# A four-layer graph network on one core: row sums of four node tiles in 32 moved to DMA, and one step of the first layer's opening moved by a unit

## The chip, the core and the metric

The kernel runs on one core of a Trainium2 chip. A core has five engines with queues of their own: PE (matrix products), DVE (vector operations), ACT (scalar functions), POOL (GpSimd) and SP (here only a queue for transfers). They run side by side and wait for each other by semaphores. Sixteen DMA engines move data between memory and the core's SBUF, fed from the queues of SP, ACT and POOL. The metric is the device time of one execution in microseconds (us). It is the median of the runs shown.

## What is computed

4096 nodes with 256 features go through four layers, each a sort of attention over the same 4096 x 4096 adjacency matrix, each followed by a residual sum and a layer norm. The change concerns the first layer:

```python
def _L0_gnn_ref(h, adj, W, a):
    Wh = (h @ W).reshape(n, heads, d)                       # 4 heads of 64
    s_i = jnp.einsum('nhd,hd->nh', Wh, a[:, :d])
    s_j = jnp.einsum('nhd,hd->nh', Wh, a[:, d:])
    e = s_i[:, None, :] + s_j[None, :, :]
    e = jax.nn.leaky_relu(e, negative_slope=0.2)
    e = jnp.where((adj == 0)[:, :, None], -jnp.inf, e)
    alpha = jax.nn.softmax(e, axis=1)
    out = jnp.einsum('ijh,jhd->ihd', alpha, Wh).reshape(n, heads * d)
    return jax.nn.elu(out)
...
x = _layernorm(x + _L0_gnn_ref(x, adj, L0_gnn_W, L0_gnn_a), axis=-1)
x = _layernorm(x + _L1_gnn_ref(...), axis=-1)
x = _layernorm(x + _L2_gnn_ref(...), axis=-1)
x = _layernorm(x + _L3_gnn_ref(...), axis=-1)
```

The weight of an edge, exp(leaky_relu(s_i + s_j)), is the larger of exp(s_i + s_j) and exp(0.2 (s_i + s_j)). A factor that depends on the row i alone drops out of the softmax. Divided by exp(0.2 s_i) it is max(exp(0.8 s_i) exp(s_j), exp(0.2 s_j)), and exp(0.2 s_j) can also be taken out of the maximum: exp(0.2 s_j) max(exp(0.8 s_i) exp(0.8 s_j), 1).

## The kernel before

**Tiles and units.** The first layer is `additive_heads`. The nodes are cut into 32 tiles of 128 (`NT`) and 8 blocks of 512 (`NB`). For a block b of rows i and a node tile j there is one unit; the loop runs over all 256 units, blocks outermost. In a unit `weights(b, j)` makes a buffer `prob` of 128 nodes j by 4 heads by 512 rows i, 1 MB in all, and `sums(b, j)` multiplies it into the block's accumulators in PSUM. `sums` follows `weights` two units later in the program (`LAG`).

**Weights.** `row[b]` holds exp(0.8 s_i) of the block's rows on all partitions, `dst` holds exp(0.8 s_j). ACT makes Relu(row x dst - 1) for each head, four operations of 128x512 (L299). DVE then adds 1 and multiplies by the edge mask for all heads, one operation of 128x2048 (L302). The mask of two units is one transfer of 512 KB on SP's queue (L295). The buffers `prob` come from the pool `zp`, which has eight.

**Sums.** `V` holds the projected features times exp(0.2 s_j), and exp(0.2 s_j) itself in its last four columns. PE holds 32 columns of V for each head and moves `prob` through: for each of three groups n four products, one a head, into 32 output partitions each (L312). Groups 0 and 1 give the features, group 2 (n = HC) takes the last columns, spread over 32 columns, and gives the row sums. A product of these 32-bit numbers leaves two records in the trace. At the end of a block ACT and DVE copy the three accumulators into `kept` (L317). In the next block's units `finish` transposes them (`turned`, L324), divides by the row sums and does elu, the residual and the layer norm (`outputs`, `add_elu` with `neg` on DVE and ACT in turn, L229 to L231).

**First block.** While it runs, `turn` transposes the next blocks' input and `prepare` projects it (`additive_values`): products L215, three exponentials on ACT (L219 to L221), and the scaled V on DVE (L222), in a group of three node tiles and a group of one. `prepare(0)`, the rows of block 0 and `turn(1)` stand ahead of the loop. After unit 0 come `turn(2)` and `prepare(1)`; from unit 3 on every fourth unit prepares one more block.

**Other queues.** Every eighth unit (j = 4, 12, 20, 28) `narrow` has POOL copy one column of that unit's `prob` into `tick` (L90) and then issue a transfer that stores a part of the adjacency matrix as bytes (`edges`, L1349). Only the second layer reads it. `rows` (L281 to L288) makes the row of the block after next by two transfers on SP's queue.

**Order.** PE's order is the program's (`manual_schedule`). In this layer a scheduler orders the other engines by the data's ways. The later layers, `multi_head_attention`, `additive_one` and `cosine_attention`, are not touched. The second layer sums its row sums in part by accumulating transfers from POOL (`den`, L873), and that is where its entries in the profile come from.

Of the kernel before, what the change touches and what calls it, by code (L numbers as in the profile page):

```python
# [9 lines left out]
FP = mybir.dt.float32  # L10
# [3 lines left out]
AF = mybir.ActivationFunctionType  # L14
OP = mybir.AluOpType
# [3 lines left out]
P = 128  # L19
D = 256  # L20
KC = D // P
QB = 4
QW = QB * P
# [5 lines left out]
def kernel(  # L29
# [27 lines left out]
    nc = tc.nc  # L57
    N = x.shape[0]
    NT = N // P
    NB = N // QW  # L60

    def pool(stack, name, bufs, **kw):
        return stack.enter_context(tc.tile_pool(name=name, bufs=bufs, reuse_waits="tile", **kw))
# [8 lines left out]
    ones = const.tile([P, P], FP, name="ones")  # L72
# [29 lines left out]
    def attach(pl, w_sb, a_sb, H):  # L102

        d = D // H
        for c in range(KC):
            prod = pl.tile([P, H, 2, d], FP, name="prod")
            nc.vector.tensor_tensor(prod, w_sb[:, c, :D].rearrange("p (h d) -> p h d", h=H).unsqueeze(2)
                                    .to_broadcast([P, H, 2, d]), a_sb.rearrange("p (h n d) -> p h n d", h=H, n=2), OP.mult)
            nc.vector.tensor_reduce(w_sb[:, c, D:].rearrange("p (n h) -> p h n", h=H), prod, AX.X, OP.add)
# [95 lines left out]

    def additive_values(xT, b, groups, w_sb, V, src, dst, H, slope):

        g = 1.0 - slope  # L210
        heads = "p k (h d) -> p k h d"
        for k, n, pw in groups:
            for c in range(KC):
                for i in range(n):
                    nc.tensor.matmul(pw[:, i, :D + 2 * H], xT[:, c, k + i], w_sb[:, c, :],  # L215
                                     start=(c == 0), stop=(c == KC - 1))
            t = slice(b * QB + k, b * QB + k + n)
            s, d = pw[:, :, D:D + H], pw[:, :, D + H:D + 2 * H]
            nc.scalar.activation(src[:, t, :], s, AF.Exp, scale=g)  # L219
            nc.scalar.activation(dst[:, t, :], d, AF.Exp, scale=g)  # L220
            nc.scalar.activation(V[:, t, D:], d, AF.Exp, scale=slope)  # L221
            nc.vector.tensor_tensor(V[:, t, :D].rearrange(heads, h=H), pw[:, :, :D].rearrange(heads, h=H),  # L222
                                    V[:, t, D:].unsqueeze(3).to_broadcast([P, n, H, D // H]), OP.mult)

# [10 lines left out]
    def additive_heads(a, H, slope, early, narrow, ahead):  # L235


        d = D // H
        G = P // H
        HC = H // 2  # L240
        MJ = 2
        mvs, kept = {}, {}
        with ExitStack() as lay:
            keep = pool(lay, "ga_keep", 1)
            V = keep.tile([P, NT, D + H], FP, name="V")
            src = keep.tile([P, NT, H], FP, name="src")
            dst = keep.tile([P, NT, H], FP, name="dst")
            w_sb = keep.tile([P, KC, D + 2 * H], FP, name="w0_sb")
# [3 lines left out]
            load_w(w_sb[:, :, :D], w0, nc.scalar)  # L252
            load_x(1)
            rp = pool(lay, "ga_row", 2)
            zp = pool(lay, "ga_z", 8)
            sb = pool(lay, "ga_sb", 2)
            mp = pool(lay, "ga_mask", 4)
            dr = pool(lay, "ga_dram", 2, space=bass.MemoryType.DRAM)
            ps = pool(lay, "ga_ps", 2, space=PSUM)
            pa = pool(lay, "ga_pa", 2, space=PSUM)  # L260
            edges = adjT.rearrange("(t p) i -> p t i", p=P)
            row, mask, acc, prob = {}, {}, {}, {}

            def bank():
                return ps.tile([P, QW], FP, name="g")
# [9 lines left out]
            def keep_rows(banks):  # L275
                for h in range(H):
                    (nc.vector.tensor_copy if h % 2 else nc.scalar.copy)(row[0][:, h, :], banks[h])
# [13 lines left out]
            def weights(b, j, rows=None):  # L291
                m = b, j // MJ
                if j % MJ == 0:
                    mask[m] = mp.tile([P, MJ, QW], I32, name="mask")
                    nc.sync.dma_start(mask[m], edges[:, j:j + MJ, b * QW:(b + 1) * QW])  # L295
                z = prob[b, j] = zp.tile([P, H, QW], FP, name="prob")
                for h in range(H):
                    r = rows[h] if rows else row[b][:, h, :]
                    nc.scalar.activation(z[:, h, :], r, AF.Relu, bias=-1.0, scale=dst[:, j, h:h + 1])  # L299
                if rows:  # L300
                    keep_rows(rows)
                nc.vector.scalar_tensor_tensor(z, z, 1.0, mask[m][:, j % MJ, :].unsqueeze(1).to_broadcast([P, H, QW]),  # L302
                                               OP.add, OP.mult)

            def sums(b, j):
                if j == 0:
                    acc[b] = pa.tile([P, HC + 1, QW], FP, name="acc")
                for n in range(HC + 1):
                    for h in range(H):
                        lo = h * d + n * G  # L310
                        part = V[:, j, lo:lo + G] if n < HC else V[:, j, D + h:D + h + 1].to_broadcast([P, G])
                        nc.tensor.matmul(acc[b][h * G:(h + 1) * G, n, :], part, prob[b, j][:, h, :],  # L312
                                         start=(j == 0), stop=(j == NT - 1))
                if j == NT - 1:
                    kept[b] = [fin1.tile([P, QW], FP, name=f"kept{c}") for c in range(HC + 1)]
                    for c in range(HC + 1):
                        (nc.vector.tensor_copy if c == 1 else nc.scalar.copy)(kept[b][c], acc[b][:, c, :])  # L317
                    mvs[b] = fin.tile([P, QB, 2], FP, name="mv")
# [35 lines left out]
            def turn(b, bank=bank):  # L354
                if b + 2 < NB:
                    load_x(b + 2)
                busy = (nc.scalar.copy if b == 0 else nc.vector.tensor_copy,
                        nc.vector.tensor_copy if b == 1 else nc.scalar.copy)
                xTs[b] = transposed_block(sb, bank, b, busy)

            def prepare(b):
                groups = [(0, HC + 1, side), (HC + 1, 1, bank().rearrange("p (n f) -> p n f", n=1))]
                additive_values(xTs[b], b, groups, w_sb, V, src, dst, H, slope)

            pos, roots, xTs = {}, {}, {}
            LAG = 2
            units = [(b, j) for b in range(NB) for j in range(NT)]
            with tc.manual_schedule(engines={mybir.EngineType.PE}):


                over = pa.tile([P, HC + 1, QW], FP, name="acc")
                side = pa.tile([P, HC + 1, QW], FP, name="acc")

                def warm(n):

                    for _ in range(n):
                        nc.tensor.matmul(over[:, 0, :P], ones, ones, start=True, stop=True)

                warm(2)
                nc.tensor.matmul(side[:, 0, :], ones[:1, :], a_row, start=True, stop=True)  # L380
                attach(keep, w_sb, side[:, 0, :], H)
                turn(0)
                warm(2)
                prepare(0)
                banks = [bank()] + [over[:, h, :] for h in range(H - 1)]
                first_rows(banks)
                free = iter([side[:, 0, :], side[:, 1, :]])
                turn(1, lambda: next(free))
                for i in range(len(units) + LAG):
                    if i < len(units):  # L390
                        b, j = units[i]
                        weights(b, j, None if i else banks)
                        if (b, j) == (1, 4 * QB):
                            early()
                        if i % 8 == 4:
                            narrow(prob[b, j][:, 0, :1])
                    if i >= LAG:
                        b, j = units[i - LAG]
                        sums(b, j)
                        if b:  # L400
                            finish(b - 1, j)

                    if i == 0 or i % QB == 3 and 3 + i // QB <= NB:
                        b = 1 if i == 0 else 2 + i // QB
                        if b + 1 < NB:
                            turn(b + 1)
                        prepare(b)
                        if b == 3:
                            rows(1, bank())
                    if i == (NB - 1) * NT + 20:  # L410
                        ahead(bank)
# [299 lines left out]
    def multi_head_attention(w_sb, b_sb, tail, rows_of_den, rows_done, narrow_edges, ga):  # L711
# [7 lines left out]
        G = P // H  # L719
        MJ = 4  # L720
        NH = N // d
# [317 lines left out]
    class Cosine:  # L1039

        MJ = 4
# [321 lines left out]
    with ExitStack() as weights1, ExitStack() as den1, ExitStack() as weights3:  # L1363
# [19 lines left out]
        def ahead(bank):  # L1383
            bm_sb["x"] = transposed_block(wp, bank, 0)
# [42 lines left out]
```

## Time and profile before

| | us |
|---|---|
| median of 3 runs | 2785.65 (2785.55 to 2785.95) |
| the profiled execution | 2785.99 |
| its span, first to last instruction | 2784.2 |
| first layer's sums on PE | 19.9 to 723.3 |
| one block of the first layer, from the second on | 84.4 |

The block's time is the distance between the first `kept` transposes of neighbouring blocks on PE, which start at 397.5 and 481.9 us. On the page each engine's first figure is the time in which it was busy. PE's weight loads (PEld) lie beside its products. A group's line gives the busy time, the mean duration in ns, then the engine's idle time ahead of it and what ended that. Durations of instructions that follow at once overlap by some 90 ns, so counts times means are more than the busy time. The tensor clock was granted at 0.999 of full speed.

### The profile page before, as it was taken

The page shows a single profiled execution, that of the slowest core. Times are in us where ns is not written, and L with a number is a line of the kernel's source. Part 1 is how long each engine was busy: PE and PEld are TensorE (multiplying, and loading weights), DVE is VectorE, ACT ScalarE, POOL GpSimd, SP SyncE. Part 2 cuts the span into 40 slices and gives each one's busy share as a digit, 9 for nine tenths or more (in the row PEclk, how much of TensorE's full clock was granted, in tenths as well). Part 3 has the DMA queues.
Part 4 walks back from the last instruction along what each step waited for, and adds up shares of the span by engine and source line. Part 5 has one row for each costly group of instructions (what it writes and reads, how often), then busy time and mean ns, then how long its engine had stood idle before and what let it go on. Part 6 is the DMA issues. An engine that isn't in the chain of part 4 may idle for free. (4 is left out here: it accounts for less than half of the span.)

```text
span 2784.2 us, 50486 instructions
## 1 busy us (share of the span) xinstructions
PE 2768.9 (99%) x19557; PEld 1449.1 (52%) x19557; DVE 2299.5 (83%) x3049; ACT 1703.4 (61%) x2668; POOL 1080.8 (39%) x1020
## 2 busy tenths in 40 slices
PE   9999999999999999999999999999999999999999
PEld 5333333333453333333333335888888777777776
DVE  8899999999677788887888878888887866777776
ACT  8899999999336666666666666465565422222222
POOL 0000100100029878778787887455455000000000
PEclk9999999999999999999999999999999999999999
DMA  7566676665339899998989988567777545445442
GB/s 207 107 142 137 139 145 124 140 143 119 69 98 192 185 176 196 193 187 186 192 181 189 190 183 188 175 197 214 186 209 230 121 69 83 76 77 83 75 72 43
DMA packets 275066, 411.94 MB, mean 148 GB/s; under 512 B 54809, under 2 KB 155657, under 8 KB 273930
## 3 DMA queue, kind: packets, MB, share of 16 engines
q0 software_dynamic: 104176, 182.74, 41.5%
q1 hardware_dynamic: 164280, 218.88, 26.2%
q10 hardware_dynamic: 6370, 7.10, 0.8%
q8 instruction: 153, 2.51, 0.4%
q14 instruction: 87, 0.71, 0.1%
HBM read 335.94 MB, written 39.40 MB: 135 GB/s over the span
## 5 line engine op out<-in xcount | busy, mean ns | idle before, releaser
L857 DVE TENSOR_TENSOR prob<-p,mask 128x1024 f32<-128x1024 f32 x512 | 619.3, 1222 | 165.3 <-ACT p L847 158.5
L847 ACT ACTIVATE p<-p,shift 128x1024 f32<-128x1024 f32 x512 | 555.5, 1087 | 319.9 <-PE p L845 318.9
L312 PE MATMUL acc<-prob,V 128*32 128x512 f32 x6144 | 664.0, 592 | 1.1 <-DVE prob L302 1.1
L299 ACT ACTIVATE prob<-row,dst 128x512 f32<-128x512 f32 x1020 | 635.0, 713 | 0.6
L302 DVE SCALAR_TENSOR_TENSOR prob<-prob,mask 128x2048 f32<-128x2048 f32 x256 | 580.3, 2285 | 25.8 <-ACT prob L299 25.1
L867 POOL TENSOR_TENSOR den<-den,prob 128x1024 f32<-128x1024 f32 x220 | 557.8, 2535 | 92.9 <-DVE prob L857 82.7
L845 PE MATMUL p<-qT,kT 64*64 64x512 f32 x4096 | 531.1, 590 | 2.6 <-DVE prob L857 2.6
L881 PE MATMUL acc<-prob,V 64*64 64x512 f32 x4096 | 529.9, 589 | 0.0
L312 PEld LDWEIGHTS acc<-prob,V 128*32 128x32 f32 x6144 | 197.3, 110 | 453.0 <-issue 431.3
L453 PE MATMUL acc<-mix,mixed 128*128 128x256 f32 x1476 | 401.4, 380 | 2.0 <-DVE quarters L475 1.0
L881 PEld LDWEIGHTS acc<-prob,V 64*64 64x64 f32 x4096 | 157.4, 133 | 282.2 <-issue 280.3
L453 PEld LDWEIGHTS acc<-mix,mixed 128*128 128x128 f32 x1476 | 278.5, 190 | 45.6 <-PE acc L453 3.1
L845 PEld LDWEIGHTS p<-qT,kT 64*64 64x64 f32 x4096 | 154.3, 133 | 279.6 <-issue 253.3
L90 POOL COPY tick<-prob 128x1 f32<-128x1 f32 x35 | 38.0, 1085 | 642.7 <-DVE prob L302 641.7
L1154 DVE TENSOR_TENSOR prob<-prob,mask 128x1024 f32<-128x1024 f32 x128 | 156.3, 1221 | 142.9 <-ACT prob L1145 142.9
L873 POOL DMA_DIRECT2D den<-prob x240 | 230.5, 961 | 61.9 <-DMA den<-prob 25.4
L453 PE MATMUL acc<-prob,X 128*128 128x256 f32 x984 | 252.6, 379 | 0.0
L1073 POOL DMA_DIRECT2D mask<-in_adjT x64 | 47.6, 743 | 526.9 <-DVE prob L1154 508.3
L453 PEld LDWEIGHTS acc<-prob,X 128*128 128x128 f32 x984 | 186.7, 190 | 78.8 <-issue 59.2
L586 DVE SCALAR_TENSOR_TENSOR prob<-r,own,mask 128x512 f32<-128x512 f32 x252 | 177.0, 743 | 48.4 <-POOL mix L445 11.4
L1145 ACT ACTIVATE prob<-p 128x512 f32<-128x512 f32 x144 | 86.1, 598 | 212.5 <-PE p L1141 212.5
L1145 ACT ACTIVATE prob<-g 128x512 f32<-128x512 f32 x112 | 66.9, 597 | 199.3 <-PE g L1141 199.3
(239 smaller groups left out, 2845.1 us busy)
## 6 DMA issues: line engine op xcount, KB each, us to landing
mask<-in_adjT SPq DMA_DIRECT2D x254, 512.0 KB
den<-prob POOLq DMA_DIRECT2D x240, 512.0 KB, 5.2
mask<-edges SPq DMA_DIRECT2D x512, 64.0 KB
mask<-in_adjT POOLq DMA_DIRECT2D x64, 512.0 KB, 5.6
edges<-in_adj POOLq DMA_DIRECT2D x32, 512.0 KB, 9.9
far<-squares SPq DMA_DIRECT2D x16, 512.0 KB
den<-prob SPq DMA_DIRECT2D x16, 512.0 KB
row<-far SPq DMA_DIRECT2D x7, 1024.0 KB
```

Of the source, the lines that this page charges most:

```text
L299: nc.scalar.activation(z[:, h, :], r, AF.Relu, bias=-1.0, scale=dst[:, j, h:h + 1])
L302: nc.vector.scalar_tensor_tensor(z, z, 1.0, mask[m][:, j % MJ, :].unsqueeze(1).to_broadcast([P, H, QW]), OP.add, OP.mult)
L312: nc.tensor.matmul(acc[b][h * G:(h + 1) * G, n, :], part, prob[b, j][:, h, :], start=(j == 0), stop=(j == NT - 1))
L453: nc.tensor.matmul(acc[at][:, half * HW:(half + 1) * HW], w, a, start=(g == 0 and n in (0, 2, 3, 5)), stop=(g == NP - 1), skip_group_check ...
L586: nc.vector.scalar_tensor_tensor(z[:, n, :], r, ga.own[:, j:j + 1], mask[:, n, :], OP.add, OP.mult)
L845: nc.tensor.matmul(p[c * d:(c + 1) * d, r, :], kT[half, c, at:at + d], qT[half, c, cols], start=True, stop=True)
L847: nc.scalar.activation(p, p, AF.Exp, bias=shift)
L857: nc.vector.tensor_tensor(z, p, mask[m][:, j % MJ, :].unsqueeze(1).to_broadcast([P, KC, QW]), OP.mult)
L867: nc.gpsimd.tensor_tensor(to, to, flat, OP.add)
L873: nc.gpsimd.dma_start(to, flat, accum_op=OP.add)
L881: nc.tensor.matmul(acc[b][c][r * d:(r + 1) * d, :], V[half, j, r * d:(r + 1) * d], prob[b, j][half, r, :], start=(j == 0), stop=(j == NH - 1))
L1154: nc.vector.tensor_tensor(z, z, co.mask[b, 2 * g // MJ][:, lo:lo + 2, :], OP.mult)
```

## The change

Four node tiles (`APART`: 3, 11, 19, 27) are treated apart.

- Their exp(0.2 s_j) is not multiplied into V; V is copied. `dst` holds exp(s_j) for them.
- ACT makes row x dst without bias or Relu (L307). DVE takes the maximum with exp(0.2 s_j) and multiplies by the mask, now head by head, four operations of 128x512 (L314), since the second operand differs from head to head.
- The whole `prob` of such a unit is then moved into `den[b]` by a transfer of 1 MB on POOL's queue. The first of a block is a plain copy, the other three accumulate.
- `sums` leaves the third group of products out for these units. At the end of the block one group of four products of ones with `den[b]` adds their row sums.
- `den` has one buffer of the size of a `prob`; `zp` has seven instead of eight.
- `turn(2)` and `prepare(1)` stand after unit 1 instead of unit 0.

```diff
-    def additive_values(xT, b, groups, w_sb, V, src, dst, H, slope):
+    def additive_values(xT, b, groups, w_sb, V, src, dst, H, slope, apart):
...
-            nc.scalar.activation(dst[:, t, :], d, AF.Exp, scale=g)
+            alone = b * QB + k in apart
+            nc.scalar.activation(dst[:, t, :], d, AF.Exp, scale=1.0 if alone else g)
             nc.scalar.activation(V[:, t, D:], d, AF.Exp, scale=slope)
+            if alone:
+                nc.vector.tensor_copy(V[:, t, :D], pw[:, :, :D])
+                continue
...
+        APART = (3, 11, 19, 27)
...
-            zp = pool(lay, "ga_z", 8)
+            zp = pool(lay, "ga_z", 7)
...
+            dp = pool(lay, "ga_den", 1)
...
                 for h in range(H):
                     r = rows[h] if rows else row[b][:, h, :]
-                    nc.scalar.activation(z[:, h, :], r, AF.Relu, bias=-1.0, scale=dst[:, j, h:h + 1])
+                    if j in APART:
+                        nc.scalar.mul(z[:, h, :], r, dst[:, j, h:h + 1])
+                    else:
+                        nc.scalar.activation(z[:, h, :], r, AF.Relu, bias=-1.0, scale=dst[:, j, h:h + 1])
                 if rows:
                     keep_rows(rows)
+                if j in APART:
+                    for h in range(H):
+                        nc.vector.scalar_tensor_tensor(z[:, h, :], z[:, h, :], V[:, j, D + h:D + h + 1],
+                                                       mask[m][:, j % MJ, :], OP.max, OP.mult)
+                    if j == APART[0]:
+                        den[b] = dp.tile([P, H, QW], FP, name="den")
+                        nc.gpsimd.dma_start(den[b], z)
+                    else:
+                        nc.gpsimd.dma_start(den[b], z, accum_op=OP.add)
+                    return
...
-                for n in range(HC + 1):
+                for n in range(HC if j in APART else HC + 1):
...
-                                         start=(j == 0), stop=(j == NT - 1))
+                                         start=(j == 0), stop=(j == NT - 1 and n < HC))
                 if j == NT - 1:
+                    for h in range(H):
+                        nc.tensor.matmul(acc[b][h * G:(h + 1) * G, HC, :], ones[:, :G], den[b][:, h, :],
+                                         start=False, stop=True)
...
-                    if i == 0 or i % QB == 3 and 3 + i // QB <= NB:
-                        b = 1 if i == 0 else 2 + i // QB
+                    if i == 1 or i % QB == 3 and 3 + i // QB <= NB:
+                        b = 1 if i == 1 else 2 + i // QB
```

More of the change, by code (lines that the diff above doesn't have):

```diff
@@ L261, in additive_heads @@
             edges = adjT.rearrange("(t p) i -> p t i", p=P)
-            row, mask, acc, prob = {}, {}, {}, {}
+            row, mask, acc, prob, den = {}, {}, {}, {}, {}
             def bank():
@@ L362, in prepare @@
                 groups = [(0, HC + 1, side), (HC + 1, 1, bank().rearrange("p (n f) -> p n f", n=1))]
-                additive_values(xTs[b], b, groups, w_sb, V, src, dst, H, slope)
+                additive_values(xTs[b], b, groups, w_sb, V, src, dst, H, slope, APART)
             pos, roots, xTs = {}, {}, {}
```

## The prediction

> **What bounds the kernel now.** I read the page from the top: its busy shares and the slices, then the dearest groups, then busy time by stage in the first layer, then the waits, and last the timeline where that layer begins and ends. From the page:
>
> ```profile
> PE 2768.9 (99%) x19557; PEld 1449.1 (52%) x19557; DVE 2299.5 (83%) x3049; ACT 1703.4 (61%) x2668; POOL 1080.8 (39%) x1020
> ...
> L312 PE MATMUL acc<-prob,V 128*32 128x512 f32 x6144 | 664.0, 592 | 1.1 <-DVE prob L302 1.1
> L299 ACT ACTIVATE prob<-row,dst 128x512 f32<-128x512 f32 x1020 | 635.0, 713 | 0.6
> L302 DVE SCALAR_TENSOR_TENSOR prob<-prob,mask 128x2048 f32<-128x2048 f32 x256 | 580.3, 2285 | 25.8 <-ACT prob L299 25.1
> ...
> den<-prob POOLq DMA_DIRECT2D x240, 512.0 KB, 5.2
> ```
>
> The tensor engine is busy 99% of the span, and its largest group is the sums of the first layer at L312: 6144 records in 664.0 us, 0.108 us each. They waited 1.1 us in all. The busy time of three source blocks of that layer, cut near their edges (columns: stretch and length, busy time and count of each engine, clock, DMA share, GB/s), and the tensor engine's waits between 100 and 720 us:
>
> ```profile
> 301.00:386.00 85.00, 85.00 (x793) 26.34 (x789) 81.73 (x71) 82.55 (x139) 7.77 (x8) 1.00 0.67 138
> 386.00:470.00 84.00, 84.00 (x781) 25.96 (x777) 80.73 (x71) 81.55 (x137) 7.77 (x8) 1.00 0.67 139
> 470.00:555.00 85.00, 85.00 (x789) 26.21 (x785) 81.74 (x71) 82.55 (x139) 7.76 (x8) 1.00 0.67 138
> ```
> ```profile
> PEld acc L312 <- DVE prob L302: 7.2, 24, 0.3
> PEld g L324 <- issue: 6.7, 8, 0.8
> PEld g L324 <- ACT prob L299: 5.0, 6, 0.8
> ```
>
> A block takes 84.4 us (the first transposes of two neighbouring blocks start at 397.5 and 481.9). PE is busy all of it, ACT 97.1%, DVE 96.1%, the DMA engines 67%. So PE sets the pace, but the next two engines have only 2.4 us (ACT) and 3.3 us (DVE) a block to give. The weight loads' waits of 0.3 us lie beside running products and cost PE nothing. How far the others are ahead is seen at the layer's end, in the timelines of PE and DVE:
>
> ```profile
> 689.65 33.68 PE L312 MATMUL acc<-prob,V 128*32 128x512 f32 x312
> 723.26 4.10 PE L755 MATMUL g<-xT,wk_sb 128*128 128x512 f32 x8
> ```
> ```profile
> 705.40 2.29 DVE L302 SCALAR_TENSOR_TENSOR prob<-prob,mask 128x2048 f32<-128x2048 f32 x1 [0.28 <-ACT prob L299]
> 707.95 0.71 DVE L129 STREAM_TRANSPOSE squares<-X 128x512 f32<-128x512 f32 x1 [0.26 <-PE acc L312]
> 724.02 0.69 DVE L317 COPY kept<-acc 128x512 f32<-128x512 f32 x1 [15.36 <-ACT kept L317]
> ```
>
> DVE finishes its last unit at 707.7, PE at 723.3: 15.6 us, six units of 2.59 us (24 x 0.108), lie finished in the eight buffers. At the start PE waits once, for the second unit:
>
> ```profile
> 19.94 2.78 PE L312 MATMUL acc<-prob,V 128*32 128x512 f32 x24
> 23.87 2.78 PE L312 MATMUL acc<-prob,V 128*32 128x512 f32 x24 [1.15 <-DVE prob L302]
> ```
>
> [...] here the row has no gaps and work taken from it should show as time, which is what I rest on, not on the 99%.[...]
>
> **The change, part by part.**
>
> 1. Row sums off PE. In units 3, 11, 19 and 27 of each of 8 blocks the third group of four products goes. A product leaves two records, so 8 records x 0.108 = 0.865 us a group: 32 groups, 27.7 us. Each block gets one such group back (ones times `den`): 8 x 0.865 = 6.9 us. Net 20.8 us, 2.6 us a block: PE needs 81.8 instead of 84.4.
>
> 2. DVE. One operation over 2048 becomes four over 512 with a pointer scalar. Back to back the long one takes 2.2 us (six in 13.38 us from 269.32). A 512-wide operation takes 0.69 us alone and 0.61 back to back (two L129 in 1.29 us at 746.91); L586, of the same form but reading PSUM beside busy POOL, takes 743 ns. So the four take between 2.4 and 2.97 us; I take 2.5, +0.3 a unit and 1.2 a block (0.8 to 3.1). The copy of V for these tiles replaces a multiply of the same size: nothing. DVE then needs 81.1 + 1.2 = 82.3 us a block.
>
> 3. ACT. A product with a scale instead of Relu with a bias, same shape. Nothing in the trace shows it from SBUF; plain copies of this width out of PSUM (L317) take 585 ns against 713. Between -1.6 us a block (16 x 0.1) and +0.5; I take 0, so 82.0 us.
>
> So PE at 81.8 is faster than ACT at 82.0 and DVE at 82.3, by some 0.5 us a block. The lead hides that: of the 15.6 us at the end only 3.5 (last unit and the row-sum group) must remain, 12 us may be used up over seven blocks, 1.7 us a block. One buffer fewer (8 to 7) takes 2.6 of it, leaving 9.5, or 1.35 a block. ACT and DVE may take up to 83.1 us a block before PE starves. In the first block PE has the projections too (112 us from 19.9 to 132), and the two others are busy only 86 and 88%: cover enough.
>
> 4. Transfers. Four of 1 MB a block on POOL's queue, three of them accumulating. In the second layer 0.5 MB takes 5.2 us from issue to landing; twice that is 10.4 us, 8 to 13 with the slim-edge transfer of the unit after (9.9 us) in the same queue. DMA engines: queue 0 in the second layer moved 115 MB in 61.9% of 1000 us, so 1 MB is 5.4 us of all sixteen: 67% rises to about 93%. Mask loads are asked for about 15 us before use and are done at least 10.5 us before use in these blocks by the packets' times; a burst of 5 to 6 us more fits. On POOL the issue (about 1 us per 0.5 MB) stands before the tick of the next unit and its edges, which only the second layer reads. The first transfer of a block must wait until PE has read the old `den`; queued behind it are that tick and the edges, and ACT waits for the tick seven units later: covered. A buffer is now held until its transfer has landed: at most 13 us, while PE with 4 units of lead frees it after about 13 as well, and ACT needs it only then. PE's new wait at the end of a block is for the transfer of unit 27: four units (10.3 us) plus the lead of 4 (10.3) against 8 to 13: hidden; if the lead were gone, up to 3 us x 8 blocks.
>
> 5. The order at the start. PE's compiled order is the same. On DVE the second unit's weights now come before the last V of block 1, an operation of 0.42 us: 0.34 back to back. PE's wait of 1.15 us falls by that, -0.3 us. V of that tile comes 2 us later, and its PSUM bank is wanted only at 26.6, by the next block's transposes, after 23.8: nothing. SP: the mask loads keep their place here; later `row<-far` stands one mask load earlier in SP's queue, up to 2 us of wait before that mask, inside the 10.5.
>
> 6. Block edges in the compiled order: between the two `neg` and the first `o<-neg` DVE now has one 0.6 us operation instead of 2.2, so it may wait some 0.4 us for ACT once a block; inside the 1.35. Near the end two transposes (`squares`, 1.3 us) move ahead of the last units, because they no longer wait for PE; PE's lead covers them, and the next layer's first turned block comes earlier, which PE doesn't wait for now (0.13 us idle from 723 to 800).
>
> Sum: -20.8 - 0.3 = -21.1 us, and I give back 0.6 for a lead that may run short in the last block: -20.5. The profiled execution took 2785.99 (span 2784.2 and 1.8 around it), 0.3 over the median: 2765.5 there, 2765.2 by the median.
>
> **Rivals.**
>
> A, ACT and DVE become the bound. For it: 97 and 96% busy, and the in-order stalls of ACT at `neg` (12.5 us between 30 and 650). Against: the lead. If the pair takes R a block, DVE, which now ends the 33rd unit at 120.0, ends the last at 120.0 + 7R and PE 3.5 later. R = 84: 711.5 instead of 723.3, so 11.8 + 0.3 saved: 2773.6 by the median. At R = 84.4 it is 2776.4.
>
> B, the row sums' transfers hold the buffers. This is the slower one. With seven buffers ACT may write a unit again only when the transfer out of it has landed. Six units of 2.56 give 15.3 us; each us of landing beyond costs 32 us, less the 31 us of lead and saving. So from 16.3 us on it is slower than before: at 17 us, 54 - 31 = +23, 2809. For it: DMA at 93%, and the edges transfer in the same queue. Against: half the size lands in 5.2 us where the DMA engines are already busy nine tenths.
>
> C, nothing gained: mask loads come late by 2 to 3 us at the bursts and the lead is used up by 32 x 1 us: 2785. Against: 10.5 us of slack.
>
> **How the numbers follow.** Forecast 0.76 (own range 2763.5 to 2768.5), A 0.14, C 0.04, B 0.06. The range runs from 2763, ACT's product at its cheap end and no loss, to 2774, A at R = 84. A measurement can tell 0.2% (5.6 us) from no change. Faster by that: forecast and A, 0.90. Within: C, 0.04. Slower: B, 0.06.
>
> **What would show it.** L312 with its ones products should lose 192 records and some 21 us. PE's last sum should come near 702.5 and PE have no idle above 1 us in the layer. DVE's last unit should lie 4 to 12 us before it: closer than 3.5 and A holds. The 512-wide operation should take 0.65 to 0.74 us. `den<-prob` of 1 MB should land in 8 to 13 us; over 15 speaks for B, and ACT would then wait for DMA. Late masks (C) would show as DVE waiting for `mask<-in_adjT`. Wrong would be a span in which PE's busy time falls by 20 us and its idle time grows as much.

## The result and the profile after: the first layer became longer

| | before | after |
|---|---|---|
| median (lowest to highest) of 4 runs, us | 2785.80 (2785.55 to 2786.64) | 2814.70 (2810.63 to 2817.81) |
| ratio, 95% interval | | 1.0101 (1.0089 to 1.0114) |
| the profiled execution, its span | 2785.99, 2784.2 | 2810.63, 2808.8 |
| PE begins the second layer | 723.3 | 744.5 |

The change makes the kernel about 1% slower; the forecast was 2765.2. The span grew by 24.6 us, and 21.3 us of it (744.5 - 723.3) had come by the end of the first layer. The other 3.3 us lie in later layers, which are the same code. These layers vary in kernels that don't touch them too: from PE's begin of the second layer to the end of the span it is 2060.9 us in the kernel before, 2065.3 in e5_seven and 2067.2 in e4_order_alone below. So the end of the first layer on PE is the measure used below.

From the page of the kernel after (busy time and mean ns ahead of the bar's end, then idle time before the group and what ended it):

```profile
PE 2770.8 (99%) x19365; PEld 1443.6 (51%) x19365; DVE 2309.7 (82%) x3145; ACT 1704.0 (61%) x2668; POOL 1234.1 (44%) x1052
...
L332 PE MATMUL acc<-prob,V 128*32 128x512 f32 x5888 | 658.3, 596 | 20.6 <-DVE prob L322 19.9
...
L309 ACT ACTIVATE prob<-row,dst 128x512 f32<-128x512 f32 x892 | 558.9, 711 | 32.2 <-DMA den<-prob 29.0
L322 DVE SCALAR_TENSOR_TENSOR prob<-prob,mask 128x2048 f32<-128x2048 f32 x224 | 505.6, 2284 | 51.8 <-ACT prob L309 51.5
...
L90 POOL COPY tick<-prob 128x1 f32<-128x1 f32 x35 | 163.0, 4657 | 98.9 <-DVE prob L322 89.9
...
den<-prob POOLq DMA_DIRECT2D x32, 1024.0 KB, 9.7
```

PE did lose its 192 records (19557 to 19365), but it is still called 99% busy and its busy time did not fall. At the 0.108 us a record of before, the 5888 records of L332 would take 636 us; 658.3 are shown as busy, so some 22 us of the loss lie inside time that the profile counts as busy. The idle columns show the rest. PE now waits 20 us for DVE, DVE 51 us for ACT, and ACT 29 us for a DMA. One line that did not matter before stands out: POOL copies the same 128x1 column, and the mean has gone from 1085 to 4657 ns. The kernel before, from its page, its list of waits (15 to 760 us: total us, times, longest us) and its list of ticks (shortest, median, longest in ns; first and last start):

```profile
L90 POOL COPY tick<-prob 128x1 f32<-128x1 f32 x35 | 38.0, 1085 | 642.7 <-DVE prob L302 641.7
DVE prob L302 <- ACT prob L299: 25.1, 100, 0.8
L90 POOL COPY tick<-prob x35: 183/315/2278, 31.1 to 2119.9; 128x1 f32<-128x1 f32 x35
```

Busy time by stage, of three source blocks of the kernel after (columns as before):

```profile
400.00:490.00 90.00, 88.09 (x784) 26.73 (x780) 82.99 (x83) 82.69 (x139) 30.36 (x12) 1.00 0.84 177
490.00:579.00 89.00, 84.48 (x751) 25.41 (x744) 80.79 (x83) 80.41 (x136) 30.34 (x12) 0.98 0.82 177
579.00:668.00 89.00, 85.58 (x759) 25.64 (x758) 81.99 (x83) 81.53 (x138) 30.38 (x12) 1.00 0.84 178
```

A block takes 89 us (the first `kept` transposes start at 400.6, 487.5 and 577.8), and no engine is busy all of it. DVE and ACT need 81 to 83 us of the 89, PE less than 89. So it is not a resource that ran out; the engines wait for each other. The waits of the kernel after between 30 and 700 us (who, for whom: total us, times, longest us) give the chain:

```profile
DVE prob L322 <- ACT prob L309: 51.5, 55, 5.1
ACT prob L309 <- DMA den<-prob: 29.0, 12, 4.8
...
PE acc L332 <- DVE prob L322: 18.2, 21, 2.7
ACT prob L307 <- POOL tick L90: 15.0, 6, 3.1
```

PE waits for DVE, DVE for ACT, and ACT for two things that did not hold it before: transfers into `den`, 29.0 us, and POOL's tick, 15.0 us. Together they are 44.0 us. The plan was an end of the layer at 723.3 - 20.8 = 702.5; it came at 744.5, so 42.0 us were lost. The two waits are of the size of the whole loss. That is a match of sums and not yet a proof: the runs below take the waits away.

Both are waits for a free `prob` buffer. There are seven, so ACT can begin a unit only when the unit seven earlier has been given up by all its readers: PE, and where they exist the transfer into `den` and the tick.

**The transfer.** POOL's timeline of the kernel after, around the start of the fourth block in 400.6 (start, us, engine, line; idle before):

```profile
395.72 0.18 POOL L90 COPY tick<-prob 128x1 f32<-128x1 f32 x1 [6.78 <-DVE prob L322]
396.21 0.76 POOL L1372 DMA_DIRECT2D edges<-in_adj  x1 [0.31 <-issue]
396.96 0.58 POOL L318 DMA_DIRECT2D den<-prob  x1
...
422.98 8.72 POOL L90 COPY tick<-prob 128x1 f32<-128x1 f32 x1 [1.15 <-DVE prob L322]
...
464.17 13.12 POOL L90 COPY tick<-prob 128x1 f32<-128x1 f32 x1 [1.49 <-DVE prob L322]
```
ACT's timeline of the same kernel:
```profile
399.17 7.46 ACT L309 ACTIVATE prob<-row,dst 128x512 f32<-128x512 f32 x12
409.70 2.56 ACT L309 ACTIVATE prob<-row,dst 128x512 f32<-128x512 f32 x4 [3.07 <-DMA den<-prob]
...
477.32 2.56 ACT L307 ACTIVATE prob<-row,dst 128x512 f32<-128x512 f32 x4 [3.01 <-POOL tick L90]
```
And DVE's:
```profile
390.30 2.73 DVE L314 SCALAR_TENSOR_TENSOR prob<-prob,V,mask 128x512 f32<-128x512 f32 x4
...
412.29 2.29 DVE L322 SCALAR_TENSOR_TENSOR prob<-prob,mask 128x2048 f32<-128x2048 f32 x1 [3.34 <-ACT prob L309]
...
420.56 11.10 DVE L322 SCALAR_TENSOR_TENSOR prob<-prob,mask 128x2048 f32<-128x2048 f32 x5
431.56 0.25 DVE L352 RECIPROCAL rden<-g 128x4 f32<-128x4 f32 x2
...
461.75 15.50 DVE L322 SCALAR_TENSOR_TENSOR prob<-prob,mask 128x2048 f32<-128x2048 f32 x7
478.08 2.74 DVE L314 SCALAR_TENSOR_TENSOR prob<-prob,V,mask 128x512 f32<-128x512 f32 x4 [0.83 <-ACT prob L307]
```

Unit 3 of the block is finished at 393.03 (390.30 + 2.73). Its transfer, L318, is issued only at 396.96: in POOL's compiled order it stands behind the tick of unit 4, which waits for DVE, and behind the 512 KB of `edges`, which are then ahead of it in the same queue. ACT goes on at 409.70, when it has landed. The buffer was held 16.7 us after DVE had finished it. ACT, which works a little ahead of DVE, asked for it at 406.63, after 13.6 us; it waits 3.07 us, DVE 3.34 us. The transfer itself took 12.7 us from issue to landing. From the second block on the first transfers of a block took 12.5 to 14.4 us, the others 8.1 to 10.6. In e12_no_tick below, with no edges between the unit and its transfer, the sixteen transfers that start between 300 and 640 us, four of them the first of a block, took 7.3 to 9.5 us.

**The tick.** The copy of one column that starts at 422.98 ends at 431.70, with the last of five DVE operations (431.66). The one of 464.17 ends at 477.29, with the last of seven (477.25), and ACT, which wants that buffer, goes on at 477.32 after 3.01 us. This is a wait in a circle: ACT stands still for the tick, the tick for DVE, and DVE's row ends only because no more units come from ACT (its next operation, at 478.08, starts after a gap of 0.83 us, `<-ACT prob L307`). All five ticks of 13.12 to 13.13 us in this kernel's first layer end so.

In the first layer of the kernel after POOL's copy waits, but for one, for the end of DVE's unbroken row of these operations: 13 of the 14 ticks above 2.3 us (6.52 to 13.13 us) end within 0.06 us of the end of such a row, and the one of 377.30 (10.92 us) ends after five operations of a row that goes on. Before, DVE waited for ACT ahead of 100 of its 256 units, for 0.16 us in the median, and no tick lasted longer than 2.28 us. Now a treated unit takes DVE 0.45 us longer, DVE is behind ACT for some units after it, gaps are gone, and just there the tick of the next unit stands. That the 0.45 us closed the gaps is read from the timelines; no run changes them alone.

The end of the layer in the timelines of PE and DVE of the kernel after, which answer to those of before:

```profile
743.57 1.04 PE L336 MATMUL acc<-den,ones 128*32 128x512 f32 x8
744.55 4.10 PE L778 MATMUL g<-xT,wk_sb 128*128 128x512 f32 x8
```
```profile
736.10 4.45 DVE L322 SCALAR_TENSOR_TENSOR prob<-prob,mask 128x2048 f32<-128x2048 f32 x2
```

DVE ends its last unit at 740.55, 4.0 us before PE. Of the lead of 15.6 us nothing is left but the last unit and the product with `den`.

### The profile page after: what moved, and what is told of

Read it like the earlier page. It is cut to its first block, busy times and chain, and to the rows that moved or that the text cites. A ratio compares the mean times of both kernels' runs of the same rounds, so it can differ in the third digit from the quotient of the medians.

```text
span 2808.8 us, 50280 instructions
## 1 busy us (share of the span) xinstructions
PE 2770.8 (99%) x19365; PEld 1443.6 (51%) x19365; DVE 2309.7 (82%) x3145; ACT 1704.0 (61%) x2668; POOL 1234.1 (44%) x1052
## 5 line engine op out<-in xcount | busy, mean ns | idle before, releaser
L332 PE MATMUL acc<-prob,V 128*32 128x512 f32 x5888 | 658.3, 596 | 20.6 <-DVE prob L322 19.9
L309 ACT ACTIVATE prob<-row,dst 128x512 f32<-128x512 f32 x892 | 558.9, 711 | 32.2 <-DMA den<-prob 29.0
L322 DVE SCALAR_TENSOR_TENSOR prob<-prob,mask 128x2048 f32<-128x2048 f32 x224 | 505.6, 2284 | 51.8 <-ACT prob L309 51.5
L332 PEld LDWEIGHTS acc<-prob,V 128*32 128x32 f32 x5888 | 190.8, 110 | 471.3 <-issue 383.7
L896 POOL DMA_DIRECT2D den<-prob x240 | 231.7, 965 | 63.5 <-DMA den<-prob 27.2
L90 POOL COPY tick<-prob 128x1 f32<-128x1 f32 x35 | 163.0, 4657 | 98.9 <-DVE prob L322 89.9
L320 POOL DMA_DIRECT2D den<-prob x24 | 21.1, 879 | 393.7 <-DVE prob L314 370.6
```

Source lines behind the costliest of these rows:

```text
L896: nc.gpsimd.dma_start(to, flat, accum_op=OP.add)
```

## The experiments

Two theories: the first transfer of a block holds its buffer too long because of its place in POOL's queue; and the tick holds its buffer too long because DVE keeps POOL out. The rivals are that accumulating transfers as such are too dear, that seven buffers are too few, and that the layer is bound by DVE and ACT. Each run was compared with the kernel before on the same chip. These medians (2789.1 to 2789.7) are some 3 us above the one of the table, so the ratios are what is to be compared.

| run | median, us | before there | ratio (95%) | PE begins layer 2, against 723.3 |
|---|---|---|---|---|
| e0_again, the kernel after | 2817.13 | 2789.16 | 1.0098 (1.0083 to 1.0113) | +29.0 |
| e1_tick_apart | 2819.82 | 2789.08 | 1.0111 (1.0095 to 1.0126) | +22.7 |
| e2_first_by_sp | 2791.24 | 2789.08 | 1.0004 (0.9997 to 1.0011) | -1.5 |
| e3_both | 2777.45 | 2789.08 | 0.9961 (0.9946 to 0.9976) | -16.5 |
| e6_no_transfers | 2787.08 | 2789.08 | 0.9996 (0.9988 to 1.0005) | -2.3 |
| e5_seven | 2788.89 | 2789.69 | 0.9998 (0.9990 to 1.0007) | -0.3 |
| e4_order_alone | 2789.09 | 2789.16 | 1.0000 (0.9991 to 1.0008) | -1.0 |
| e8b_pause | 2778.83 | 2789.16 | 0.9963 (0.9949 to 0.9978) | -14.7 |
| e7_edges_later | 2771.90 | 2789.69 | 0.9940 (0.9925 to 0.9955) | -18.5 |
| e12_no_tick | 2771.96 | 2789.69 | 0.9939 (0.9922 to 0.9956) | -19.8 |

The last column is from one profiled execution each. That of the kernel after differs by 8 us between its two profiles, so a few us there mean little where its waits are present.

### The tick alone, the first transfer alone, both

**e1_tick_apart**: DVE copies the column into a tile of its own, and POOL's tick reads that. The tick lasts nearly as long as in the kernel after (mean 4.47 against 4.66 us) but no longer holds a `prob` buffer.

```diff
-            with behind(z):
+            seen = fin.tile([P, 1], FP, name="seen")
+            nc.vector.tensor_copy(seen, z)
+            with behind(seen):
```

> The changed kernel, but POOL's tick no longer reads prob: DVE copies one column into a small tile and POOL's copy reads that, so a buffer isn't held while POOL's copy is locked out. Theory T (the tick, starved while DVE runs two-input operations back to back, holds the buffers): ACT's 15 us of waits for the tick in the first layer go and the time falls from 2814.7 to about 2800. Theory D (the transfers into den hold them): within 4 us of 2814.7, and the waits for DMA den<-prob stay at about 29 us. Theory E (ACT, DVE and PE are simply too evenly loaded): within 4 us as well, and both kinds of wait turn into others.

**e2_first_by_sp**: the plain transfer of a block goes by SP's queue, past POOL's tick and edges.

```diff
-                        nc.gpsimd.dma_start(den[b], z)
+                        nc.sync.dma_start(den[b], z)
```

> The changed kernel, but each block's first transfer into den, the plain copy, goes by SP's queue, where no edges transfer stands ahead of it. Theory D: ACT's 29 us of waits for den<-prob fall to under 8 and the time to 2788 to 2797. Theory T: at most 5 us off, since the tick still holds its buffers. Theory E: within 4 us of 2814.7.

**e3_both**: the two edits together.

> Both edits together. D and T both true and one after the other in the block: about 44 us off, 2771, and PE ends the first layer near 705. If only one of them matters: no better than the better one of the two alone. Theory E: above 2805.

Waits of e1, 15 to 760 us:

```profile
ACT prob L309 <- DMA den<-prob: 41.0, 13, 6.1
```
Waits of e2 in the same stretch:
```profile
ACT prob L307 <- POOL tick L90: 18.3, 6, 3.1
...
PE acc L332 <- DVE prob L322: 8.1, 15, 0.9
```
Waits of e3:
```profile
PE acc L332 <- DVE prob L322: 3.7, 6, 0.9
```

Each edit takes away the wait that it was aimed at and no other. With both, ACT no longer waits for the tick, and for transfers 1.7 us in all. But the two don't add up in a simple way. From the kernel after, e2 takes 22.8 us off the first layer (21.3 + 1.5; 30.5 against that kernel's second profile) and e1 nothing that can be told, so the 2800 us that the tick alone would have given in e1 did not come; from e2, the edit of e1 takes another 15.0 us. The layer then ends at 706.8, near the 705 expected. In e1 the waits for transfers grow to 41.0 us. The buffers are used in turn, so when ACT is no longer stopped at one of them, it arrives earlier at the next that is held, and waits there. The longest wait of ACT for a transfer is 4.8 us in the kernel after and 6.1 us in e1. Only when the later hold is gone as well does the first removal show as time.

### The transfers as such

**e6_no_transfers** has a constant tile in place of `den` and no transfers. It leaves out the row sums of the four tiles; every other operation stays, the product with ones too.

```diff
-                    if j == APART[0]:
-                        den[b] = dp.tile([P, H, QW], FP, name="den")
-                        nc.gpsimd.dma_start(den[b], z)
-                    else:
-                        nc.gpsimd.dma_start(den[b], z, accum_op=OP.add)
+                    den[b] = still
```

> The changed kernel without any transfer into den: den is set to one value once, so the row sums of the four tiles are left out, and everything else is as it was. It shows what the engines' load alone gives, with the tick as it was. Theory D: the time falls by at least 29 us, to 2786 or below. Theory T: by less than 10. Theory E: by less than 5. If the transfers' descriptors or traffic slow anything else, it falls by more than 29.

Waits of e6:

```profile
ACT prob L309 <- POOL tick L90: 18.4, 6, 3.1
```

The first layer ends 0.8 us earlier than in e2, and the ratios' intervals overlap. The tick's wait is there without any transfer into `den` (18.4 us, in e2 18.3), so it isn't a result of these transfers. That the 32 transfers, 24 of them accumulating, cost nothing is not shown by this pair alone: the tick holds ACT in both, and could hide a cost, as in e1. e7 and e12 below show it. They have all 32 transfers, ACT waits no more than 1.0 us for them in the first layer, and it ends 18.5 and 19.8 us earlier than before, out of the 21.1 us of the sum.

### One buffer fewer, and the order at the start

**e5_seven** is the kernel before with seven buffers:

```diff
-            zp = pool(lay, "ga_z", 8)
+            zp = pool(lay, "ga_z", 7)
```

> The kernel before with seven buffers instead of eight, nothing else. If one buffer fewer costs by itself: PE ends the first layer later than 723.3 us and the time rises by 2 us or more. If it only takes 2.6 us of the lead, as predicted: PE still ends it within 0.5 us of 723.3, and the time is unchanged within 2 us.

**e4_order_alone** is the kernel before with the second block's turn and products after unit 1:

```diff
-                    if i == 0 or i % QB == 3 and 3 + i // QB <= NB:
-                        b = 1 if i == 0 else 2 + i // QB
+                    if i == 1 or i % QB == 3 and 3 + i // QB <= NB:
+                        b = 1 if i == 1 else 2 + i // QB
```

> The kernel before with turn(2) and prepare(1) behind unit 1, and nothing of the row sums. Prediction's step 5: PE's one wait of 1.15 us in the opening falls to 0.7 to 0.9, PE ends the first layer 0.2 to 0.5 us before 723.3, and the time is unchanged within its spread. If the new order costs: later than 723.5.

PE's opening in e4:

```profile
22.92 2.78 PE L312 MATMUL acc<-prob,V 128*32 128x512 f32 x24 [0.83 <-DVE prob L302]
```

Neither changes the time by anything that can be told. Seven buffers are enough where each is given up in time. PE's second unit waits 0.83 us in place of 1.15: the 0.3 us of the forecast, too small for a median to show.

### DVE and the tick

**e8b_pause** asks whether it is DVE's unbroken run that keeps POOL out. It is e2 with a short DVE operation that reads nothing, put behind each unit that has a tick:

```diff
+                            with tc.issue_after(getattr(last, "ins", last)):
+                                nc.vector.memset(pause, 0.0)
```

> The kernel with the first transfer by SP, and a write of a constant to 128x256 (no input, some 0.3 us) on DVE right behind the unit whose column POOL's tick copies. If POOL's copy is locked out by DVE's two-input operations: the tick's mean falls from 4.7 to under 1 us, ACT's 18 us of waits for the tick go, and PE ends the first layer at 708 to 714 instead of 721.8, though DVE has 10 us more to do in all. If the tick is slow for another reason: its mean stays above 4 us and the layer ends no earlier than 721.

All ticks of e8b (shortest, median, longest in ns; first and last start):

```profile
L90 POOL COPY tick<-prob x35: 175/2324/2330, 31.1 to 2107.5; 128x1 f32<-128x1 f32 x35
```
And of e0_again:
```profile
L90 POOL COPY tick<-prob x35: 182/2200/13132, 31.6 to 2149.9; 128x1 f32<-128x1 f32 x35
```

An earlier form, e8_pause, which kept its 128x256 tile for the whole kernel, left 23.75 KB a partition in SBUF where the second layer takes 24 KB, and gave no time.

The longest tick falls from 13.13 to 2.33 us, ACT no longer waits for it, and the first layer ends 13.2 us before that of e2. So in these two runs what DVE runs decides how long the tick lasts. That it is the two inputs of DVE's operation that matter, as the expectation has it, was its author's assumption; no run changes the inputs alone. The expectation of ticks below 1 us on average was missed, with 1.47 us: most still take one whole DVE operation. The timelines of e8b around one of them, DVE's and POOL's:

```profile
445.01 0.27 DVE L421 MEMSET pause<- 128x256 f32 x1
445.21 13.23 DVE L323 SCALAR_TENSOR_TENSOR prob<-prob,mask 128x2048 f32<-128x2048 f32 x6
```
```profile
445.14 2.33 POOL L90 COPY tick<-prob 128x1 f32<-128x1 f32 x1 [1.48 <-DVE prob L323]
```

The copy starts beside the memset and is shown until 447.47, the end of the first of six operations that follow without a gap. In the kernel after a copy that started within such a row waited, but for one, for the row's end, and one that started 0.03 us ahead of an operation (395.72) took 0.18 us. Why a copy that starts just ahead of the row comes through after one operation here isn't settled by these runs.

### Two versions that avoid both

**e7_edges_later** is the kernel after with the tick and the edges two units later, a change of one number:

```diff
-                        if i % 8 == 4:
+                        if i % 8 == 6:
```

> The changed kernel with tick and edges two units later (units 6, 14, 22, 30 instead of 4, 12, 20, 28). The first transfer of a block stays on POOL's queue but now stands ahead of the edges in it. If it is the place behind the edges that makes it late: ACT's waits for den<-prob fall from 29 us to under 10 and PE ends the first layer near 722, as with SP's queue, instead of 744.6. If it is POOL's path as such: it ends within 5 us of 744.6.

**e12_no_tick** has no tick in the first layer. The edges follow each transfer into `den` in POOL's order:

```diff
-                        nc.gpsimd.dma_start(den[b], z)
+                        moved = nc.gpsimd.dma_start(den[b], z)
                     else:
-                        nc.gpsimd.dma_start(den[b], z, accum_op=OP.add)
+                        moved = nc.gpsimd.dma_start(den[b], z, accum_op=OP.add)
+                    narrow(moved)
...
-                        if i % 8 == 4:
-                            narrow(prob[b, j][:, 0, :1])
...
-            with behind(z):
+            with tc.issue_after(getattr(z, "ins", z)):
```

> The changed kernel without the ticks: the edges transfers stand on POOL's queue right behind the four transfers into den, whose wait for DVE paces them. Both suspected holds go at once, with nothing added on DVE and nothing on SP. If the two holds are the whole loss: no waits of ACT for den<-prob or tick above 5 us in all, PE ends the first layer at 703 to 708 (744.6 with the change), and the time is 12 to 18 us below before. If the accumulating transfers hold buffers as well: above 712.

Busy time of two blocks of e7, and then its POOL timeline:

```profile
304.00:387.00 83.00, 83.00 (x770) 25.70 (x762) 81.61 (x83) 81.34 (x138) 21.54 (x12) 1.00 0.90 191
387.00:469.00 82.00, 82.00 (x761) 25.49 (x760) 80.77 (x82) 80.30 (x137) 21.54 (x12) 1.00 0.91 189
```
```profile
447.74 8.72 POOL L90 COPY tick<-prob 128x1 f32<-128x1 f32 x1 [5.89 <-DVE prob L322]
...
459.64 0.54 POOL L318 DMA_DIRECT2D den<-prob  x1 [2.45 <-PE acc L332]
466.40 0.18 POOL L90 COPY tick<-prob 128x1 f32<-128x1 f32 x1 [6.22 <-DVE prob L322]
```

PE is busy without a gap again. The first transfer now stands ahead of the next tick and its edges. It is issued 0.6 us after DVE has finished the unit (459.64 and 459.07) and lands 10.9 us later, though the edges issued at 456.40 are still under way in the same queue. Ticks of 8.72 us still occur; here they end before ACT needs the buffer, and ACT waits for none. So this edit took away both holds: 722 us was expected for the end of the layer, as in e2, and it came at 704.7. The ends of the first layer, in e7 and in e12:

```profile
703.77 1.04 PE L336 MATMUL acc<-den,ones 128*32 128x512 f32 x8
704.74 4.10 PE L778 MATMUL g<-xT,wk_sb 128*128 128x512 f32 x8
```
```profile
702.54 1.04 PE L337 MATMUL acc<-den,ones 128*32 128x512 f32 x8
703.51 4.10 PE L777 MATMUL g<-xT,wk_sb 128*128 128x512 f32 x8
```

Both beat both kernels: 0.994 of the time before. Which of the two is better can't be told.

## Why the prediction was wrong

The sign was wrong. The sum of the work was right; the step that failed is the fourth, on what holds a buffer.

1. **Row sums off PE: right.** In e7, where PE doesn't starve, the first `kept` transposes start at 304.79, 386.61 and 468.43 us: 81.82 us a block, against 81.8 predicted and 84.4 before.

2. **DVE: right in kind, too small.** Where four 512-wide operations stand in a row, the next unit follows 2.65 us after their start (456.34 to 458.99 in e7), against 2.20 us for one 2048-wide operation: +0.45 us a unit and 1.8 a block, where 1.2 was taken out of a range of 0.8 to 3.1. DVE's copies of `kept` in e7 lie 83.1 us apart, so the pair of DVE and ACT needs 83.1 a block and not 82.3. That is the very limit up to which the lead was said to last, and it just did: DVE ends its last unit at 700.7 in e7, PE at 704.7. What the step did not ask is what else DVE's gaps were good for. The tick was running in them.

3. **ACT: right.** L307 takes 713 ns and L309 711.

4. **Transfers: the step that failed.** It said that a buffer is held "until its transfer has landed: at most 13 us", and that ACT needs it only then. The landing was forecast at 8 to 13 us: the median is 9.7, but four of the eight first transfers, those that mattered, took 13.1 to 14.4. Two things were wrong in the hold.
   - The place in the queue. The step had the first transfer wait for PE, with the tick and the edges "queued behind it". The compiled order has them ahead of it. DVE finishes the unit at 393.03, the issue is at 396.96, and with 12.7 us of landing the hold is 16.7 us, over the 13 of the step. e2 takes that order away, and with it 22.8 us of the first layer.
   - The tick as a second holder. The step saw that ACT waits for it seven units later and called that covered; it gave the tick's own duration no thought. That grew to 13.12 us. Taking its hold away is worth 15.0 us once the first is gone (e2 to e3).

   The other parts of the step held. DMA share was 0.90 in e7, with 0.93 expected; no DVE operation waited for a mask in the steady blocks; the accumulating transfers cost nothing that can be told (e7, e12).

5. **The order at the start: right,** 0.3 us, shown alone by e4.

6. **Block edges:** not tried alone. In e12, which has all the edges of the change, the first layer ends 19.8 us earlier than before, so with the 21.1 us of the sum some 1.3 us at most seem to have gone there and into the short lead at the end.

**Rivals.** B, held buffers, was the right one, with a chance of 0.06. Its mechanism, a buffer that isn't free in time, was right, and so was its sign that ACT would wait for DMA. Its cause was not: it looked for slow landing under DMA load in all 32 units, and its turning point of 16.3 us rests on that; the runs don't test it. The holds were long by the order of one queue, once a block, and by a copy on POOL. A, ACT and DVE as the bound, is refuted as the cause of the loss: in e7 they carry the same work and PE doesn't starve. C, late masks, did not happen: no DVE operation waits for a mask.

**What stays open.** Between its first layer and its end, a kernel's gain or loss changes by several us. Against before, e1 ends the first layer 22.7 us late and is 30.7 us slower by the medians; e3 is 16.5 us early there and 11.6 us faster, e12 19.8 and 17.7. The ends of the layer are from single profiles on different chips, so a part of this can be spread. The later layers are the same code; what moves them wasn't tried. Nor was `den` with eight buffers, or DVE's longer unit alone.

## What to carry to other kernels

A buffer is held by its slowest reader, counted from when it is written to when that reader is done: the wait for a turn in a queue, the issue and the landing, for each reader. Here that was 16.7 us for a transfer that landed 12.7 us after its issue, and up to 13.13 us for a copy of one column. Before a buffer is given a new reader or the pool is made smaller, write that sum down for all of them, and take the order of the queue from the compiled program, not from the source. And where the gaps of a nearly full engine are to be filled with work, look first for what was running in these gaps: here a copy that took at most 2.28 us before and up to 13.13 us after.

## What the runs showed of the hardware

That a copy of one column on POOL takes 0.18 us or 13.12 us in the same kernel, depending on what DVE runs beside it, was not expected. L322 reads `prob` and `mask`, and the tick reads `prob`. In the first layer of the kernel after each of the 14 ticks above 2.3 us started within an unbroken row of L322 and waited, but for one, for the end of the row: seven of them for four operations (8.72 us), five for six (13.12 or 13.13 us). The tick of 732.89, which started beside L129 with L322 following only at 733.30, took 0.18 us. In e8b, with a memset ahead of the row, no tick lasted longer than 2.33 us, one operation. Why the copy waits isn't shown: no run changes what DVE's operation reads alone. What ends the wait isn't settled either. It need not be a gap: at 431.56 L352 follows at once, which reads what PE wrote. And in e7 the tick of 447.74 ends at 456.46, just as L314 follows at once, which reads `prob` and `mask` as L322 does.

A hold that is removed need not show: e1 took away 15 us of waits of ACT and gained nothing that can be told, since the wait at the next hold in the same ring of buffers grew from 29.0 to 41.0 us.
